# Reordering the q products of a single-head attention, with its statistics and quarter sums moved between engines

## Chip, cores and metric

The kernel runs on one core of one Trainium2 chip. The metric is the device time in microseconds (us) of one execution; the figure compared is the median of several runs. Everything is in float32.

## What is computed

The input is 8 samples of 512 channels by 1024 positions. Layer 0 is a group norm, an attention of 8 heads and an output projection, added to its input. Layer 1 takes that sum x, normalizes it over the whole sample, and does an attention with one head of 512 channels, again added to its input. The part of layer 1 that matters here is

```python
m, v = mean and variance of x over channels and positions
h = (x - m) / sqrt(v + eps) * gamma + beta
q = wq @ h + bq ;  k = wk @ h + bk ;  s = q.T @ k
```

The kernel does not form k: it multiplies x by one matrix made once from wq and wk (`wqk1`, with gamma on its rows and columns), and the product is what the code calls q. The mean and deviation of the sample enter afterwards, so the products of x can start before the statistics of x are known. The values are treated likewise with a product of wo and wv (`wvo1`).

## The kernel before

All samples go through the same stages one after the other. The program is written out by hand for three engines: TensorE (the matmuls), ScalarE and VectorE take their instructions in the order in which the code issues them (`manual_schedule`). Stages are generators that yield once for each product, and `at_steps(generator, hooks)` calls further work at numbered steps of it; a hook's instructions are thus put into each engine's order behind those of its step. GpSimd's and the sync engine's (SP's) instructions are placed by the framework's scheduler.

**Products by sevens.** A product of matrices split 2x2 is done with seven half-size products instead of eight (Strassen's way). The left factor gives A11, A12, A22 and the sums S1 to S4, the right one B11, B21, B22 and T1 to T4. `finish` (L195) and `Combined.make` (L436, 128x1024 subtractions on VectorE, 1.22 us each) make the S and T of weights and of x. Some of the half-size products are split by sevens again, into quarter products; their sums are made by `sums_a` (L513) for weights and by `quarters_in_steps` and `quarters_b` (L530, L536) for x and its T: per block one subtraction of 128x512 and two of 128x256.

**The projection of layer 0** (`project`, from L1257) computes four chunks of 128 channels by two halves of the positions, in ten steps; two chains, c = 0 and 1, alternate. Its half-size products are the matmuls `ps_p` at L679; a product of one chain is four rows of 128x512 in the profile. ScalarE copies a product to SBUF (`u_p`, L461), VectorE adds the next one to it (L1284) and adds the result with the bias to x (L1267). Behind some of these additions ScalarE passes twice over the 128x512 block of x just done for its mean and its sum of squares (`norm.moments`, L335): six of the eight blocks here, each right behind its addition in ScalarE's order, the other two in the next stage. `ready.halve("B22")` hangs on step 7 and `ready.halve("B21")` on the addition of chunk 3, half 0.

**Layer 1's q** (`make_q`, L1350 on) follows. It has six half-size products, called lines here: A11·B11, S2·T2 and S3·T3 for two column groups r = 0 and 1 (L679 `ps_l_q`, four matmuls of 128x512), and 14 quarter products (L1373, four matmuls of 128x256): seven named f for A12·B21 + S4·B22, seven named s for S1·T1 + A22·T4. A line owns one PSUM tile of two banks of pool "o" for the whole stage and uses its first bank; the quarter products take turns in two banks of pool "s". ScalarE copies (L1377) or VectorE adds (L1361) each quarter product. `take(r)` (L1394) adds the first line's bank to the f sums, `c12_of(r)` (L1398) adds the bank once S2·T2 is in it, and `final` (L1388) and one ScalarE pass (L1432) write q. The order of the products is

```
line0 A11, f0, f1, line1 A11, f2 .. f6, line0 S2, line1 S2, s0 .. s6, line0 S3, line1 S3
```

The statistics of the sample are put together meanwhile. `both_halves` (L352 to L358) is a chain of small operations on GpSimd, `mean_of_all` a tiny matmul (L307, `ps_m`) with a VectorE reduction (L309) and three GpSimd operations (L365 to L369), `deviation` another tiny matmul (`ps_v`), a VectorE operation (L374) and one on GpSimd (L375). The two tiny matmuls take a bank of their own (`room`).

**The values** (`ps_s_v`, `ps_o_v` at L937, `ps_l_v` at L694) come next, with the weights `w_wvo` and their quarter sums loaded by DMA (`WeightTwice("wvo1")`).

**The head, sample 0 only.** `wqk1` is scaled by gamma in place by eight VectorE operations (`scale_both`, L241), then gets its S sums (`finish`, L195) and its quarter sums (L513, `wqk_twice`), between the q, k and v products of layer 0. The last of these are spread over the v products by the list `over`. `waiting[0].finish` does the S sums of the first v weights, which VectorE begins once they are loaded.

Of the kernel before, what the change touches and what calls it, by code (L numbers as in the profile page):

```python
# [46 lines left out]
P = 128  # L47
# [18 lines left out]
def two_attention_blocks(  # L66
# [133 lines left out]
    class Weight:  # L200
# [34 lines left out]
                for _, a in self.moving(cc):  # L235
                    nc.scalar.activation(a, a, AF.Identity, scale=vec[:, by + cc : by + cc + 1])

        def scale_both(self, by, row):
            for cc in range(NC):
                for to, a in self.moving(cc):  # L240
                    nc.vector.scalar_tensor_tensor(  # L241
                        a, a, vec[:, by + cc : by + cc + 1], row[:, to], ALU.mult, ALU.mult
                    )

        def finish(self):
            for parts, rest in zip(self.parts, self.rest):
# [273 lines left out]
            engine.tensor_tensor(q[f"T{n}"], q[x], q[y], ALU.subtract)  # L520
        return q

    def quarters_in_steps(part, t):

        q = {f"B{n}": v for n, v in halve(part, lambda i, j: (i, j)).items()}
        t = (t if len(t.shape) == 2 else flat(t)).rearrange("p (n q) -> p n q", n=4)
        q.update({f"T{n + 1}": t[:, n, :] for n in range(4)})

        def first():
            nc.vector.tensor_tensor(  # L530
                t[:, 0:4:2, :], part[:, :, 2 * P :],
                part[:, 0, :].rearrange("p (n q) -> p n q", n=2), ALU.subtract,
            )

        def rest(n, x, y):
            nc.vector.tensor_tensor(q[n], q[x], q[y], ALU.subtract)  # L536

        return q, [first, lambda: rest("T2", "B22", "T1"), lambda: rest("T4", "B21", "T2")]

    def quarters_b(part, t):  # L540

        q, steps = quarters_in_steps(part, t)
        for step in steps:
            step()
        return q
# [5 lines left out]
    class WeightTwice:  # L551
# [3 lines left out]
        def __init__(self, name, make=None, later=None):  # L555
            tiles = [flat(tile2(f"{name}_twice_{n}")) for n in range(2)]
            key, self.tiles = f"{name}_twice", tiles
            if make is None:

                nc.scalar.dma_start(tiles[0], stored[key][:, : 8 * P])  # L560
                nc.scalar.dma_start(tiles[1], stored[key][:, 8 * P :])
                return
            stored[key] = dram.tile([P, 16 * P], FP, tag=key, name=f"stored_{key}")

            def step(n, i, a):
                sums_a(self.quarters(a, make), tiles[n][:, i * 4 * P : (i + 1) * 4 * P])
# [387 lines left out]
    def layer0(bs, qs, ks, b, norm_next):  # L954
# [302 lines left out]
        bias = made["bias0"]  # L1257

        later, ready = [], Ready(xs, b)

        def project(w, c):
            def done(i, half, bank, u):
                chunk = c + 2 * i
                x = piece(xs, chunk, half)

                def add():
                    nc.vector.scalar_tensor_tensor(  # L1267
                        x, bank if u is None else u, bias[:, chunk : chunk + 1], x, ALU.add, ALU.add
                    )
                    if i == half or i == 1:  # L1270
                        norm.moments(chunk, half, i == half)
                    if (i, half, c) == (1, 0, 1):
                        ready.halve("B21")


                first = last and i == half == 0
                if first and c == 0:
                    ps_sum = spares[0]
                    add_keys(end, [1], ps_sum)
                    combine1()  # L1280
                    combine2(2, 0)
                    combine2(3, 0)
                if u is not None:
                    nc.vector.tensor_tensor(u, bank, u, ALU.add)  # L1284
                if not first:
                    add()
                    return
                later.append(add)
                if c == 0:
                    invs[end] = one_over(ps_sum, f"0_{b}_{end}_1")  # L1290
                    divide(end, 1, invs[end])
                else:

                    held(flat(accs[end, 1]), f"acc_0_{b}_{end}", flat(accs[end, 1]))
                    for n, k in [(2, 1), (3, 1), (4, 0), (4, 1)]:
                        combine2(n, k)
                    for more in later:
                        more()

            return strassen(by_channels(w, c, comb), done, f"p_0_{b}_{c}")  # L1300

        w = next_weight().parts[0]
        hooks = {} if last else {2 * n - 3: [lambda n=n: combine2(n, 1)] for n in range(2, 5)}
        hooks[0] = [ready.load]
        hooks[7] = [lambda: ready.halve("B22")]
        at_steps(together(project(w, 0), project(w, 1)), hooks)
        if last:
            held(invs.pop(end), f"inv_0_{b}_{end}_1")
# [2 lines left out]
    class Ready:  # L1311


        def __init__(self, xs, b):
            self.combine, self.quarters, self.b = Combined(f"1_{b}"), {}, b
            self.combine.take(xs)

        def load(self):
            self.weights = WeightTwice("wqk1")

        def halve(self, name):
            self.quarters[name] = quarters_b(
                self.combine.parts[name], tile2(f"{name}_twice_{self.b}")
            )

    def attention1(xs, norm, ready, b, at_values):
# [23 lines left out]
        def make_q(w):  # L1350
# [4 lines left out]
            lines = [banks("o", f"ps_l{r}_q_1_{b}")[:, 0, :] for r in range(2)]  # L1355

            def pair(products, to, name):
                line, single = (banks("s", f"ps_{name}{n}_q_1_{b}")[:, 0, :] for n in range(2))
# [22 lines left out]
                    yield  # L1381

            def multiply(r, a, v, fresh):
                by_channels(w.parts[0], r, bs)(lines[r], a, v, fresh)

            def final(r, i, half, x, y):
                n = r + 2 * i
# [3 lines left out]

            def take(r):
                c11 = first[r][:, 0, :]
                nc.vector.tensor_tensor(c11, lines[r], c11, ALU.add)  # L1394

            def c12_of(r):
                c12 = first[r][:, 1, :]
                nc.vector.tensor_tensor(c12, lines[r], c12, ALU.add)  # L1398

            quarters = pair(PAIRS_Q[0], first, "f")  # L1400

# [21 lines left out]
            quarters = pair(PAIRS_Q[1], second, "s")  # L1423
            for n in range(7):
                next(quarters)
                if n == 2:
                    c12_of(0)
                if n == 4:
                    c12_of(1)
                yield  # L1430
            for r in range(2):
                nc.scalar.activation(  # L1432
                    piece(qs, r, 0), first[r][:, 0, :], AF.Identity, bias=norm.c[:, r : r + 1]
                )
                final(r, 0, 1, second[r][:, 0, :], first[r][:, 1, :])
            for r in range(2):
                multiply(r, "S3", "T3", False)
                for n, half in enumerate([1, 0]):
                    final(r, 1, half, lines[r], second[r][:, n, :])
                yield  # L1440
# [12 lines left out]
        bias = norm.bias()  # L1453

# [392 lines left out]
    made, throughs, over = {}, [], []  # L1847


    with tc.manual_schedule(engines={PE, ACT, DVE}):  # L1850
# [13 lines left out]
        gamma_row = tile2("gamma_row")[:, 0, :]  # L1864
        nc.sync.dma_start(gamma_row, gamma1.to_broadcast([P, C]))

        class Through(Rows):

# [15 lines left out]
                        nc.vector.tensor_tensor(t, t, vec[:, V_NW1 : V_NW1 + NC], ALU.mult)  # L1884

        def through_v():
            throughs.append(Through(wvo1, bias_v, wo1, "v", room("rows_v", 0)))
            wvo1.scale_rows(V_NW1, range(1))

        def through_q():  # L1890
            throughs.append(Through(wqk1, bias_q, nk1, "q", room("rows_q", 0)))
            wqk1.scale_both(V_NW1, gamma_row)

        def channels_of(half, ccs):
            for cc in ccs:
# [464 lines left out]
```

## Time and profile before

Times before are the median of 3 runs, from 2837.11 to 2839.54.

| | |
|---|---|
| median time | 2837.94 us |
| the profiled execution's own time | 2840.35 us |
| its span in the profile | 2838.6 us |
| granted TensorE clock, mean | 0.999 |
| VectorE busy | 2136.5 us, 75% |
| ScalarE busy | 1166.5 us, 41% |
| GpSimd busy | 299.3 us, 11% |
| projection of the second sample | 594.2 to 619.6 us |
| its q | 619.6 to 644.0 us |
| its values' weight products | 644.0 to 667 us |

The windows in the last three rows were read off the timeline. In them the engines were busy as follows (us):

| | length | TensorE | VectorE | ScalarE | GpSimd |
|---|---|---|---|---|---|
| projection | 25.4 | 24.45 | 14.67 | 10.06 | 0.00 |
| q | 24.4 | 24.35 | 21.94 | 11.31 | 4.75 |
| values | 23.0 | 23.00 | 16.96 | 4.68 | 0.00 |

How to read it: PE is TensorE, PEld its weight loads, DVE is VectorE, ACT ScalarE, POOL GpSimd. A line of the timeline has the start, the duration, the engine, the line of the kernel and the operation with output and inputs; "x4" joins four instructions, and the bracket says how long the engine had been idle and what released it. Matmuls overlap one another and their ends are modelled, so a group's duration runs over the start of the next one.

### The profile page before, as it was taken

The numbers are of one execution on the slowest core, as the hardware profiler recorded it, in microseconds if no ns is written. First come the engines' busy times: TensorE is split into PE (matmuls) and PEld (weight loads), VectorE is DVE, ScalarE is ACT, GpSimd is POOL, SyncE is SP. The second block draws the span as 40 slices with busy tenths as digits, with TensorE's granted clock in tenths as the row PEclk, the third lists the DMA queues.
The fourth block names the chain that finished last, engine by engine and source line by source line (L and its number), as shares of the span: only waits on it lengthen the run. The fifth ranks groups of instructions, "written<-read, shape, count | busy, mean of one in ns | idle before, by whom it ended". The sixth has DMA issues, their size and how long they took to land.

```text
span 2838.6 us, 39373 instructions
## 1 busy us (share of the span) xinstructions
PE 2817.4 (99%) x15688; PEld 1582.2 (56%) x15688; DVE 2136.5 (75%) x2963; ACT 1166.5 (41%) x1752; POOL 299.3 (11%) x316
## 2 busy tenths in 40 slices
PE   9999999999999999999999999999999999999999
PEld 5435765357643576445773466734667346673375
DVE  6776796767867778776777777777777777867777
ACT  2464224633256332553325533264332643326522
POOL 0000220003100040000400004000040000400021
PEclk9999999999999999999999999999999999999999
DMA  8523131331323313133131231313212142121001
GB/s 287 184 75 104 49 128 64 87 104 53 112 68 90 100 69 106 53 91 123 56 108 49 83 123 56 108 49 101 105 64 100 50 124 82 64 105 38 23 16 39
DMA packets 83864, 247.50 MB, mean 87 GB/s; under 512 B 21816, under 2 KB 22616, under 8 KB 77272
## 3 DMA queue, kind: packets, MB, share of 16 engines
q1 hardware_dynamic: 73768, 209.75, 22.5%
q10 hardware_dynamic: 9904, 35.16, 3.8%
q8 instruction: 125, 2.05, 0.3%
q14 instruction: 67, 0.55, 0.1%
HBM read 188.02 MB, written 33.03 MB: 78 GB/s over the span
## 4 chain that ended last, share of the span: by engine, by line
PE 85%; DVE 9%; DMA 3%; ACT 1%; issue 1%; SPq 0%; ACTq 0%; DVEq 0%
PE s L991 15%; PE ps_o L1010 15%; PE ps_o L1674 7%; PE ps_v L694 7%; PE ps_l_qk L916 4%; PE ps_l L1510 4%; PE ps_s L1493 4%; PE ps_s_qk L909 3%; PE ps_l_q L679 3%; PE ps_l_v L694 3%; PE ps_s L1510 3%; PE ps_o_qk L909 3%; PE ps_s_v L937 2%; PE ps_s_q L1373 2%; PE ps_p L679 2%; PE ps_s_two L1804 2%
## 5 line engine op out<-in xcount | busy, mean ns | idle before, releaser
L845 ACT ACTIVATE p<-s 128x1024 f32<-128x1024 f32 x512 | 523.3, 1024 | 329.6 <-PE s L991 322.7
L847 DVE TENSOR_TENSOR acc<-acc,p 128x1024 f32<-128x1024 f32 x384 | 469.8, 1223 | 99.7 <-ACT p L845 91.3
L1010 PE MATMUL ps_o<-p,v 64*64 64x512 f32 x4096 | 529.0, 589 | 0.0
L991 PE MATMUL s<-c_q,c_k 64*64 64x512 f32 x3584 | 465.3, 591 | 0.0
L1010 PEld LDWEIGHTS ps_o<-p,v 64*64 64x64 f32 x4096 | 156.7, 133 | 282.8 <-issue 278.0
L991 PEld LDWEIGHTS s<-c_q,c_k 64*64 64x64 f32 x3584 | 134.7, 133 | 253.2 <-issue 236.1
L1674 PE MATMUL ps_o<-t_p,s_v 128*128 128x512 f32 x384 | 168.2, 595 | 0.0
L352 POOL TENSOR_TENSOR part<-part,stat 128x4 f32<-128x4 f32 x8 | 3.6, 454 | 1443.6 <-ACT mean L335 1443.6
L847 DVE TENSOR_TENSOR acc<-p,p 128x1024 f32<-128x1024 f32 x64 | 78.3, 1224 | 79.2 <-ACT p L845 79.2
L1484 ACT ACTIVATE p<-p,factor 128x512 f32<-128x512 f32 (+1 forms) x112 | 85.3, 780 | 115.9 <-DVE p L1520 91.4
L1498 ACT COPY p<-ps_s 128x512 f32<-128x512 f32 x96 | 53.1, 588 | 178.3 <-PE ps_s L1493 178.3
L1674 PEld LDWEIGHTS ps_o<-t_p,s_v 128*128 128x128 f32 x384 | 72.4, 190 | 91.2 <-issue 89.1
L679 PE MATMUL ps_p<-t_p,w_p 128*128 128x512 f32 x256 | 114.7, 596 | 8.3 <-DVE u_p L1284 6.7
L1520 DVE TENSOR_TENSOR p<-ps_l,p 128x512 f32<-128x512 f32 x136 | 89.9, 683 | 39.9 <-PE ps_l L1510 39.6
L461 ACT COPY u_v<-ps_v 128x512 f32<-128x512 f32 x48 | 28.1, 585 | 205.4 <-PE ps_v L694 173.3
L1520 DVE TENSOR_TENSOR p<-ps_s,p 128x512 f32<-128x512 f32 x112 | 74.8, 685 | 37.7 <-PE ps_s L1510 37.7
L694 PE MATMUL ps_v<-w_v,t_again 128*128 128x256 f32 x448 | 99.0, 379 | 0.0
L694 PEld LDWEIGHTS ps_v<-w_v,t_again 128*128 128x128 f32 x448 | 85.2, 190 | 11.5
L1284 DVE TENSOR_TENSOR u_p<-ps_p,u_p 128x512 f32<-128x512 f32 x48 | 33.0, 687 | 76.5 <-ACT u_p L461 76.5
L679 PEld LDWEIGHTS ps_p<-t_p,w_p 128*128 128x128 f32 x256 | 48.0, 190 | 72.7 <-issue 54.2
L694 PE MATMUL ps_v<-w_v,x 128*128 128x256 f32 x384 | 86.8, 379 | 0.0
L679 PE MATMUL ps_p<-o,w_p 128*128 128x512 f32 x192 | 86.7, 594 | 0.0
(501 smaller groups left out, 5087.3 us busy)
## 6 DMA issues: line engine op xcount, KB each, us to landing
x<-in_x SPq DMA_DIRECT2D x92, 512.0 KB, 6.5
w_qk<-stored_qk SPq DMA_DIRECT2D x14, 1792.0 KB, 7.1
w_wqk<-stored_wqk SPq DMA_DIRECT2D x8, 1792.0 KB, 7.2
fold<-acc SPq DMA_DIRECT2D x56, 256.0 KB, 3.1
qk_twice<-stored_qk_twice ACTq DMA_DIRECT2D x28, 512.0 KB, 6.0
w_wvo<-stored_wvo SPq DMA_DIRECT2D x8, 1792.0 KB, 8.9
out<-x SPq DMA_DIRECT2D x28, 512.0 KB, 4.8
w_v<-stored_v SPq DMA_DIRECT2D x7, 1792.0 KB, 7.1
```

What stands on the lines that cost most here:

```text
L679: nc.tensor.matmul(bank, w[a][:, k, c * P : (c + 1) * P], bs[b][:, k, :], start=fresh and k == 0, stop=k == 1, skip_group_check=True,)
L694: nc.tensor.matmul(bank[:, u * 2 * P : (u + 1) * 2 * P], bs[b][:, k, n * P : (n + 1) * P], w[a][:, k, :], start=fresh and u == k == 0, sto ...
L845: nc.scalar.activation(p, s, AF.Exp, scale=factor)
L847: nc.vector.tensor_tensor(acc, first, p, ALU.add)
L909: nc.tensor.matmul(bank[:, i * 2 * P : (i + 1) * 2 * P], parts[a][x], twice_b[v][y], start=start and i == 0, stop=True, skip_group_check=True,
L916: nc.tensor.matmul(bank, of(i, a)[:, k, :], bs[v][:, k, :], start=start and k == 0, stop=k == 1, skip_group_check=True,)
L991: nc.tensor.matmul(s[cols, j, :], ks[pair][k0 // HALF][rows, k0 % HALF : k0 % HALF + HD], qs[pair][g][rows, :], start=True, stop=True,)
L1010: nc.tensor.matmul(o[cols, half, :], vs[kt][rows, c0 : c0 + HD], p[rows, j, :], start=kt == 0, stop=kt == NT - 1,)
L1493: nc.tensor.matmul(bank, bs[v][:, k, t * P : (t + 1) * P], q_parts[a][:, k, :], start=a == "A11" and k == 0, stop=k == 1, skip_group_check ...
L1510: nc.tensor.matmul(bank[:, u * 2 * P : (u + 1) * 2 * P], v[y][:, u * P : (u + 1) * P], a[x], start=start and u == 0, stop=True, skip_group ...
L1520: nc.vector.tensor_tensor(at(r, t), bank, at(r, t), ALU.add)
L1674: nc.tensor.matmul(bank, v_parts[kt // 2][a][:, kt % 2, c * P : (c + 1) * P], p_parts[kt // 2][b][:, kt % 2, cols], start=fresh and kt == ...
```

## The change

- Statistics: `done` no longer passes over x behind each addition. The pass is put on a list (`due`), and `ready.measure(n)` takes n from it at the projection's steps 1, 2, 7, 8 (two), 9 (two) and q's step 1.
- Quarter sums: those of B22, B21 and T1 are done by GpSimd; T1's at q's step 2 (was 9). T4's stay on VectorE, at step 8 (was 10).
- The T blocks of x: T1 and T2 at q's step 1 (were 2 and 3), T3 at 3 (was 12).
- q's order: the lines stand between the quarter products,

```
line0 A11, f0, f1, line1 A11, f2, f3, f4, line0 S2, f5, f6, line0 S3, s0, s1, s2, line1 S2, s3 .. s6, line1 S3
```

- The tiny matmuls of mean and deviation use the second bank of the lines' tiles. The mean is taken at step 8 (was 9), the deviation at 11 (was 10), the weights of the values' quarter sums are loaded at step 10 (was 8), `both_halves` moves from 3 to 2.
- Head: `wqk1` is scaled by ScalarE (rows) and GpSimd (columns), its quarter sums that were put off go to GpSimd, the load of the gamma row is issued at another place, and the S sums of the first v weights come ahead of those of `wqk1`.

```diff
-        def scale_both(self, by, row):
+        def scale_columns(self, row):
             for cc in range(NC):
                 for to, a in self.moving(cc):
-                    nc.vector.scalar_tensor_tensor(
-                        a, a, vec[:, by + cc : by + cc + 1], row[:, to], ALU.mult, ALU.mult
-                    )
+                    nc.gpsimd.tensor_tensor(a, a, row[:, to], ALU.mult)
...
-                sums_a(self.quarters(a, make), tiles[n][:, i * 4 * P : (i + 1) * 4 * P])
+                sums_a(
+                    self.quarters(a, make), tiles[n][:, i * 4 * P : (i + 1) * 4 * P],
+                    nc.vector if later is None else nc.gpsimd,
+                )
...
-                    if i == half or i == 1:
-                        norm.moments(chunk, half, i == half)
+                    due.append(lambda: norm.moments(chunk, half, i == half))
...
-        hooks[0] = [ready.load]
-        hooks[7] = [lambda: ready.halve("B22")]
+        for n, counts in [(1, 1), (2, 1), (7, 1), (8, 2), (9, 2)]:
+            hooks.setdefault(n, []).append(lambda n=counts: ready.measure(n))
+        hooks[2].append(ready.load)
+        hooks[7].append(lambda: ready.halve("B22"))
...
+        def measure(self, n):
+            for _ in range(n):
+                self.due.pop(0)()
...
-        def halve(self, name):
+        def halve(self, name, engine=nc.gpsimd):
             self.quarters[name] = quarters_b(
-                self.combine.parts[name], tile2(f"{name}_twice_{self.b}")
+                self.combine.parts[name], tile2(f"{name}_twice_{self.b}"), engine
             )
...
             yield from line(1, "A11", "B11", True)
-            for n in range(5):
-                next(quarters)
-                if n == 0:
-                    take(0)
-                if n == 4:
-                    take(1)
-                yield
+            yield from some(quarters, 2)
+            take(0)
+            yield from some(quarters, 1)
             yield from line(0, "S2", "T2", False)
+            c12_of(0)
+            yield from some(quarters, 2)
+            yield from line(0, "S3", "T3", False)
+            take(1)
+            quarters = pair(PAIRS_Q[1], second, "s")
+            yield from some(quarters, 3)
             yield from line(1, "S2", "T2", False)
...
+            yield from some(quarters, 1)
+            c12_of(1)
+            yield from some(quarters, 2)
...
+            finals(0)
+            yield from some(quarters, 1)
+            multiply(1, "S3", "T3", False)
+            finals(1)
+            yield
...
-            1: [lambda: norm.moments(0, 1, False)],
-            2: [lambda: combine.make(1), lambda: norm.moments(1, 1, False)],
-            3: [lambda: combine.make(2), norm.both_halves],
+            1: [lambda: ready.measure(1), lambda: combine.make(1), lambda: combine.make(2)],
+            2: [lambda: ready.halve("T1"), norm.both_halves],
+            3: [lambda: combine.make(3)],
             6: [lambda: combine.make(4)],
-            8: [lambda: twice_w.append(WeightTwice("wvo1"))],
-            9: [norm.mean_of_all, lambda: ready.halve("T1")],
-            10: [norm.deviation, lambda: ready.halve("T4")],
-            12: [lambda: combine.make(3)],
-            14: [norm.untaken],
+            8: [lambda: spare(1), norm.mean_of_all, lambda: ready.halve("T4", nc.vector)],
+            10: [lambda: twice_w.append(WeightTwice("wvo1"))],
+            11: [lambda: spare(0), norm.deviation],
+            15: [norm.untaken],
...
-            7: [wqk1.finish], 8: [waiting[0].finish], 9: [
+            7: [waiting[0].finish], 8: [wqk1.finish], 9: [
```

More of the change, by code (lines that the diff above doesn't have):

```diff
@@ L521, in sums_b, with quarters_in_steps @@
         return q
-    def quarters_in_steps(part, t):
+    def quarters_in_steps(part, t, engine=nc.vector):
         q = {f"B{n}": v for n, v in halve(part, lambda i, j: (i, j)).items()}
@@ L529, in first @@
         def first():
-            nc.vector.tensor_tensor(
+            engine.tensor_tensor(
                 t[:, 0:4:2, :], part[:, :, 2 * P :],
@@ L535, in rest, with quarters_b @@
         def rest(n, x, y):
-            nc.vector.tensor_tensor(q[n], q[x], q[y], ALU.subtract)
+            engine.tensor_tensor(q[n], q[x], q[y], ALU.subtract)
         return q, [first, lambda: rest("T2", "B22", "T1"), lambda: rest("T4", "B21", "T2")]
-    def quarters_b(part, t):
-        q, steps = quarters_in_steps(part, t)
+    def quarters_b(part, t, engine=nc.vector):
+        q, steps = quarters_in_steps(part, t, engine)
         for step in steps:
@@ L1259, in layer0 @@
         later, ready = [], Ready(xs, b)
+        due = ready.due
         def project(w, c):
@@ L1316, in __init__ @@
             self.combine.take(xs)
+            self.due = []
+        def measure(self, n):
+            for _ in range(n):
+                self.due.pop(0)()
         def load(self):
             self.weights = WeightTwice("wqk1")
-        def halve(self, name):
+        def halve(self, name, engine=nc.gpsimd):
             self.quarters[name] = quarters_b(
-                self.combine.parts[name], tile2(f"{name}_twice_{self.b}")
+                self.combine.parts[name], tile2(f"{name}_twice_{self.b}"), engine
             )
@@ L1354, in make_q @@
             first, second = ([tile2(f"{n}_q_1_{b}_{r}") for r in range(2)] for n in ["c11", "c22"])
-            lines = [banks("o", f"ps_l{r}_q_1_{b}")[:, 0, :] for r in range(2)]
             def pair(products, to, name):
@@ L1383, in multiply @@
             def multiply(r, a, v, fresh):
-                by_channels(w.parts[0], r, bs)(lines[r], a, v, fresh)
+                by_channels(w.parts[0], r, bs)(lines[r][:, 0, :], a, v, fresh)
             def final(r, i, half, x, y):
@@ L1393, in take, with finals @@
                 c11 = first[r][:, 0, :]
-                nc.vector.tensor_tensor(c11, lines[r], c11, ALU.add)
+                nc.vector.tensor_tensor(c11, lines[r][:, 0, :], c11, ALU.add)
             def c12_of(r):
                 c12 = first[r][:, 1, :]
-                nc.vector.tensor_tensor(c12, lines[r], c12, ALU.add)
+                nc.vector.tensor_tensor(c12, lines[r][:, 0, :], c12, ALU.add)
+            def finals(r):
+                final(r, 0, 1, second[r][:, 0, :], first[r][:, 1, :])
+                for n, half in enumerate([1, 0]):
+                    final(r, 1, half, lines[r][:, 0, :], second[r][:, n, :])
             quarters = pair(PAIRS_Q[0], first, "f")
@@ L1413, in make_q @@
             yield from line(1, "A11", "B11", True)
-            for n in range(5):
-                next(quarters)
-                if n == 0:
-                    take(0)
-                if n == 4:
-                    take(1)
-                yield
-            yield from line(0, "S2", "T2", False)
-            yield from line(1, "S2", "T2", False)
[L1423 to L1430, printed above, removed]
+            yield from some(quarters, 2)
+            take(0)
+            yield from some(quarters, 1)
+            yield from line(0, "S2", "T2", False)
+            c12_of(0)
[4 more added lines that the diff above has]
+            yield from some(quarters, 3)
+            yield from line(1, "S2", "T2", False)
+            yield from some(quarters, 1)
+            c12_of(1)
+            yield from some(quarters, 2)
             for r in range(2):
@@ L1434, in make_q, with spare @@
                 )
[L1435 to L1440, printed above, removed]
+            finals(0)
[3 more added lines that the diff above has]
+            yield
+            spares.clear()
+        def spare(r):
+            spares[:] = [lines[r][:, 1, :]]
+        lines = [banks("o", f"ps_l{r}_q_1_{b}") for r in range(2)]
         at_steps(make_q(w), {
-            1: [lambda: norm.moments(0, 1, False)],
-            2: [lambda: combine.make(1), lambda: norm.moments(1, 1, False)],
-            3: [lambda: combine.make(2), norm.both_halves],
+            1: [lambda: ready.measure(1), lambda: combine.make(1), lambda: combine.make(2)],
+            2: [lambda: ready.halve("T1"), norm.both_halves],
+            3: [lambda: combine.make(3)],
             6: [lambda: combine.make(4)],
-            8: [lambda: twice_w.append(WeightTwice("wvo1"))],
-            9: [norm.mean_of_all, lambda: ready.halve("T1")],
-            10: [norm.deviation, lambda: ready.halve("T4")],
-            12: [lambda: combine.make(3)],
-            14: [norm.untaken],
+            8: [lambda: spare(1), norm.mean_of_all, lambda: ready.halve("T4", nc.vector)],
+            10: [lambda: twice_w.append(WeightTwice("wvo1"))],
+            11: [lambda: spare(0), norm.deviation],
+            15: [norm.untaken],
         })
@@ L1845, in all_good @@
         nc.vector.tensor_copy(flag, ps[0:1, 0:1])
-    made, throughs, over = {}, [], []
+    made, throughs, over, gamma_row = {}, [], [], []
     with tc.manual_schedule(engines={PE, ACT, DVE}):
@@ L1863, in two_attention_blocks @@
         norm = norm0(xs_next, 0)
-        gamma_row = tile2("gamma_row")[:, 0, :]
-        nc.sync.dma_start(gamma_row, gamma1.to_broadcast([P, C]))
         class Through(Rows):
@@ L1886, in through_v @@
         def through_v():
+            gamma_row.append(tile2("gamma_row")[:, 0, :])
+            nc.sync.dma_start(gamma_row[0], gamma1.to_broadcast([P, C]))
             throughs.append(Through(wvo1, bias_v, wo1, "v", room("rows_v", 0)))
@@ L1891, in through_q @@
             throughs.append(Through(wqk1, bias_q, nk1, "q", room("rows_q", 0)))
-            wqk1.scale_both(V_NW1, gamma_row)
+            wqk1.scale_rows(V_NW1)
+            wqk1.scale_columns(gamma_row[0])
         def channels_of(half, ccs):
```

## The prediction

> **What bounds the kernel now.** I read the page's busy shares and its chain first:
>
> ```profile
> PE 2817.4 (99%) x15688; PEld 1582.2 (56%) x15688; DVE 2136.5 (75%) x2963; ACT 1166.5 (41%) x1752; POOL 299.3 (11%) x316
> ...
> PE 85%; DVE 9%; DMA 3%; ACT 1%; issue 1%; SPq 0%; ACTq 0%; DVEq 0%
> ```
>
> TensorE is the bound and GpSimd nearly idle. The matmuls stay the same in number and shape, so only time in which TensorE stands still can be won. Second, the table of TensorE's waits (total us, times, longest):
>
> ```profile
> PE ps_p L679 <- DVE u_p L1284: 6.7, 7, 1.2
> PE ps_l_v L694 <- DVE c_v L630: 2.0, 1, 2.0
> ...
> PE ps_l_q L679 <- DVE u_p L1284: 0.9, 6, 0.2
> ```
>
> The first row is the projection, the third the seam from it to q; both are stages the change edits. Since ends of matmuls are modelled, I size stalls by the starts of PE rows instead. In an unbroken stretch four 128x512 passes take 1.715 us (614.18 to 615.89), 0.429 each; quarter passes (128x256) come to 0.216. The second sample's projection is 56 passes, 24.04 us dense, but lasts 594.18 to 619.64, 25.46. Its q is 24 x 0.429 + 56 x 0.216 = 22.39 dense, but lasts 24.38. So 1.42 and 1.99 us are lost per sample. Third, the timeline of the larger hole:
>
> ```profile
> 601.05 1.88 PE L679 MATMUL ps_p<-t_p,w_p 128*128 128x512 f32 x4
> ...
> 601.50 0.72 ACT L335 ACTIVATE square<-x,stat 128x512 f32<-128x512 f32 x1
> ...
> 602.41 0.58 ACT L461 COPY u_p<-ps_p 128x512 f32<-128x512 f32 x1
> 603.03 0.69 DVE L1284 TENSOR_TENSOR u_p<-ps_p,u_p 128x512 f32<-128x512 f32 x1 [2.38 <-ACT u_p L461]
> ...
> 603.77 1.55 PE L679 MATMUL ps_p<-t_p,w_p 128*128 128x512 f32 x3 [0.84 <-DVE u_p L1284]
> ```
>
> The copy that frees the bank sits behind mean and square of x (600.75 to 602.32), its add behind it, TensorE behind the add. The next product should start 1.715 us after 601.05 (602.77, less a late step of the modelled start); start by start I find 1.11 us lost here. Fourth, VectorE at the end of the projection:
>
> ```profile
> 616.72 0.69 DVE L530 TENSOR_TENSOR B_twice<-x 128x512 f32<-128x512 f32 x1
> 617.44 0.89 DVE L536 TENSOR_TENSOR B_twice<-x,B_twice 128x256 f32<-128x256 f32 x2
> 618.24 0.75 DVE L1267 SCALAR_TENSOR_TENSOR x<-ps_p,bias,x 128x512 f32<-128x512 f32 x1
> 618.90 0.68 DVE L1284 TENSOR_TENSOR u_p<-ps_p,u_p 128x512 f32<-128x512 f32 x1
> ```
>
> B22's quarter sums hold back the add for which q's first product waits. Fifth, TensorE in q:
>
> ```profile
> 619.64 1.98 PE L679 MATMUL ps_l_q<-x,w_wqk 128*128 128x512 f32 x4 [0.15 <-DVE u_p L1284]
> ...
> 623.34 1.98 PE L679 MATMUL ps_l_q<-x,w_wqk 128*128 128x512 f32 x4
> ...
> 628.84 1.13 PE L1373 MATMUL ps_f_q<-B_twice,w_wqk 128*128 128x256 f32 x4
> ...
> 633.64 0.39 PE L307 MATMUL ps_v<-spread,in_sample 128*128 128x4 f32 x2
> ```
>
> A group that comes late shows some 0.1 us of extra duration. The holes before these groups: 0.32 (plus 0.10 in the first pass), 0.25, 0.26, 0.50; smaller ones of 0.08 to 0.24 make the rest of the 1.99.
>
> **The statistics on ScalarE.** Removed from ahead of the copies: a pair of passes, 1.57 us (600.75 to 602.32). With the new order ScalarE's copy can start right after the product, 5.35 us into the projection, and its add ends at about 7.75, while TensorE needs it at 8.58: the hole goes. Over samples 0 to 6 it is 1.24, 1.11, 1.12, 0.96, 1.45, 1.30, 1.36, sum 8.5. In the last sample ScalarE's order still has two pairs ahead of the copy, so its 1.26 us hole stays, as do 0.95 us behind the reciprocal. The passes themselves cost nothing where they go: ScalarE is busy 10.1 of 25.4 us in this stage. But what is queued behind them is q's copies at steps 8, 9 and 1; at 0.58 us each they come every 0.86 us or slower, so I take zero. If that cover is gone, a product that reuses the bank waits up to 1.57 once per sample.
>
> **Quarter sums to GpSimd.** B22, B21 and T1 leave VectorE: 0.69 + 0.89, some 1.5 us each. B22's removal takes the 0.32 us at the seam: 8 x 0.32 = 2.5. Together with B21's it also takes q's first 0.10 and the 0.25 before the second half-size product, whose add is then ready about 0.95 us into q, against 3.44. On GpSimd one set is 1.27 (128x512, its row by shape) + 2 x 0.73 = 2.73 us. B21's are then ready 1.3 to 2.7 us into q, and needed at 5.16. T1's come behind B21's, and ahead of both_halves on GpSimd's queue: the means are there at 8.2 to 8.7, needed by the mean's matmul at 10.3. Margin 1.6 at worst, cost zero; that matmul is in TensorE's queue, so a miss stops everything behind it.
>
> **The new order of q.** VectorE, from q's start: the last four adds of the projection (about 0.68 each when queued), T1 and T2 (1.16 each), an add (0.6), T3 (1.16), then the take (0.7): 7.5 us. The half-size S2 product waits for that take and is due at 1.715 x 2 + 0.863 x 5 = 7.75. So 0.2 us of slack, no more. What remains in q if this holds: two tiny matmuls at 0.22 (the 0.50 at the deviation falls to that, as its GpSimd input now has longer), and 0.1, 0.08, 0.1 at reused banks, 0.73 together. The moved DMA of wvo1 (two steps later) is used after q, over 8 us later than either place, against a 6.0 us row for the like load: nothing. After q, the v stage needs the bank of VectorE's last final at 5.34 us after the last quarter product, and gets it at 5.0 to 5.2: nothing.
>
> **What GpSimd beside VectorE costs.** The trace of before has the pair only in the last sample's v stage, where GpSimd's sums of S and A lie beside VectorE's:
>
> ```profile
> 2727.85 0.94 DVE L513 TENSOR_TENSOR S_twice<-s_q 128x256 f32<-128x256 f32 x1
> ...
> 2729.59 1.20 DVE L635 TENSOR_TENSOR c_v<-c_v,c_v 128x512 f32<-128x512 f32 x1
> ...
> 2731.45 4.57 PEld L694 LDWEIGHTS ps_l_v<-w_wvo,t 128*128 128x128 f32 x14 [2.35 <-DVE c_v L630]
> ```
>
> Alone these take 0.42 and 0.69; beside GpSimd each is about 0.5 longer, and TensorE waited 2 us. The Trainium skill, SBUF — State Buffer, section "SBUF: two separate sides", speaks against the change: VectorE with two SBUF inputs and GpSimd share a port pair as an exclusive lock, the loser blocked for the other's whole instruction. By the rule the two sets inside q (5.46 us), less 1.2 beside sums read from PSUM (L1520's 0.68 is not longer near GpSimd), block VectorE for 4.3 us. By the row it is 0.5 us for each VectorE sum that overlaps. Exposed at the take are T2 and T3: by the row 0 to 1.0, less the 0.2 of slack, 0.8 at the S2 product; by the rule 4.1. I side with the row, since it is the same pair of operations, and take its middle, 0.4, with 0.05 for the quarter product before it. A gain is excluded. So q loses 0.73 + 0.45 = 1.18 per sample, 9.6 over eight (rounded up), from 7 x 1.99 + 2.65 = 16.6 before. Gain 7.0; 10.7 with no contention.
>
> **The head, once.** Scaling wqk1 leaves VectorE (8 x 0.40 = 3.2 us) and the wqk_twice sums too (16 x 0.27 = 4.3), but the latter stood behind the v add (67.30) for which TensorE waited 0.5 us. Now w_v's finish (2.5 us) stands ahead of wqk1's in VectorE's queue and waits for the load that before was issued at 54.8 and landed at 60.4; it is issued somewhat earlier, so I estimate 57.3 to 59.9. From landing, two finishes, the adds and the qk sums end 10.9 later with the v add: 68.2 to 70.8, where it ended at 67.98. Six c_q issues now pass ahead on SP (about 1.1 us each there), inside that estimate. Bounds -0.6 and +7 (3.8 of it blocking by GpSimd's wqk sums); I take +2.
>
> **Sum.** -8.5 - 2.5 - 7.0 + 2 = -16. The profiled execution took 2840.35 (span 2838.6), the median run 2837.94. 2840.35 - 16 = 2824; in terms of the median 2822.
>
> **The rivals.** No contention: GpSimd's sums fall beside adds from PSUM. -8.5 - 2.5 - 10.7 + 0 = -21.7, 2816. For it: most of VectorE's work there reads PSUM. Against: three 1024-wide combines lie exactly under T1's sums.
>
> Half given back: VectorE's chain slips 1.2 us per sample, q gains nothing, the head loses 3: -8, 2830. For it: 0.2 us of slack at the take.
>
> Slower, one mechanism: the lock in full. T1's GpSimd sums block T2 or T3, the take comes 4.3 us late, and TensorE stands 4.1 before the S2 product in each sample. q then loses 8 x (0.73 + 4.1) = 38.6, 22 more than before: -11 + 22 + 2 = +13, 2851. It decides from a stall of about 2.5 us per sample there (q then eats the 11 - 2 won elsewhere). Against: the rows show 0.5 a sum, not whole instructions.
>
> Or the change doesn't do what it says: each hole reopens behind the next wait on the same bank, 2837. Against: the walk leaves 0.8 us at the large hole.
>
> **Chances.** Likeliest case 0.60 (2816 to 2828), no contention 0.14, half given back 0.15, hole reopens 0.06, slower 0.05. A measurement can tell about 0.2%, 5.7 us, from no change: faster is below 2832.3. Half given back lies mostly below it, and the reopened holes within: faster 0.87, same 0.08, slower 0.05. Range 2811 to 2831: the likeliest, most of no contention and about half of half given back, 0.8.
>
> **What would show it.** Right: the row of ps_p behind u_p shrinks to about one wait (the last sample's), projection lengths near 24.1 us, q near 23.5, VectorE's combines in q at 1.2 to 1.7. Wrong: a new row of ps_l_q waiting for DVE c_q, or ps_l_q behind POOL stat; combines above 2; ps_v waiting over 2 us at 68 to 71.

## The result, and the profile after

The changed kernel takes 2828.71 us (median of 8 runs, 2827.51 to 2830.19); in the same series the kernel before takes 2838.61 (8 runs, 2836.96 to 2841.15). The ratio is 0.9965, with a 95% interval of 0.9954 to 0.9976: 9.9 us faster, clear of no change, and inside the forecast range. The forecast was 16 us. The profiled executions took 2840.35 before and 2828.29 after (spans 2838.6 and 2825.7), so what follows explains 12.9 us of span.

The table of TensorE's waits, after (total us, times, longest), is the first view to set beside the one of before:

```profile
PE ps_v L695 <- DVE v L729: 4.3, 1, 4.3
PE ps_l_v L695 <- DVE c_v L631: 1.9, 1, 1.9
PE ps_q L680 <- DVE q L712: 1.8, 1, 1.8
...
PE ps_p L680 <- ACT u_p L459: 1.2, 1, 1.2
...
PE ps_v L695 <- DVE q L712: 0.9, 1, 0.9
```

The rows of the projection and of q behind VectorE are gone; the last sample's wait for ScalarE's copy stays. But three rows, each occurring once, are new or grown (`ps_v` behind `v` was 0.2 us before): they belong to the head of sample 0, and together are 7.0 us. (Lines moved by the change: L680 here is L679 before, L1285 is L1284, L1380 is L1373.)

The sum by stages, each measured from the first matmul of one to the first of the next (us, all samples; dense length as in the prediction):

| stage | idle or slow before | after | difference |
|---|---|---|---|
| projections, 8 | 12.8 | 2.4 | -10.5 |
| q, 8 | 16.6 | 7.6 | -9.0 |
| values of the last sample | 3.7 | 2.0 | -1.7 |
| head, to the first projection (start at 246.36, then 255.02) | | | +8.7 |
| sum | | | -12.5 |

That leaves 0.4 us elsewhere. The row of the values is a difference of the granted clock between two executions, and no gain of the change (shown further down); without it the stages give -10.8, against the medians' -9.9. Each projection of samples 0 to 6 now lasts 24.03 us (one, the third, 24.51), each q 23.33 (the last 23.38). The timeline of ScalarE in the second sample's projection shows why:

```profile
605.57 0.58 ACT L459 COPY u_p<-ps_p 128x512 f32<-128x512 f32 x1 [2.85 <-PE ps_p L680]
606.95 0.63 ACT L333 ACTIVATE mean<-x 128x512 f32<-128x512 f32 x1 [0.79 <-DVE x L1269]
```

The copy starts as soon as TensorE has released the bank, and mean and square come behind it. TensorE in the same window, as two rows without a bracket, did not stop:

```profile
603.65 3.60 PE L680 MATMUL ps_p<-o,w_p 128*128 128x512 f32 x8
607.09 4.45 PE L680 MATMUL ps_p<-t_p,w_p 128*128 128x512 f32 x10
```

The busy time of the engines over q of that sample, after (columns: length, then TensorE, weight loads, VectorE, ScalarE, GpSimd with their counts, granted clock, DMA share and GB/s):

```profile
624.25:647.58 23.33, 23.33 (x86) 15.32 (x85) 18.37 (x29) 9.18 (x20) 10.73 (x17) 1.00 0.35 124
```

In q VectorE fell from 21.94 to 18.37 and GpSimd rose from 4.75 to 10.73. VectorE's and GpSimd's rows at the start of that q show what the two do to each other:

```profile
626.22 1.63 DVE L434 TENSOR_TENSOR t<-x,x 128x1024 f32<-128x1024 f32 x1
627.89 1.23 DVE L434 TENSOR_TENSOR t<-x,t 128x1024 f32<-128x1024 f32 x1
629.03 0.68 DVE L1368 TENSOR_TENSOR c_q<-ps_f_q,c_q 128x512 f32<-128x512 f32 x1
629.64 1.84 DVE L434 TENSOR_TENSOR t<-x,x 128x1024 f32<-128x1024 f32 x1
631.40 0.68 DVE L1401 TENSOR_TENSOR c_q<-ps_l_q,c_q 128x512 f32<-128x512 f32 x1
```

```profile
624.92 1.86 POOL L534 TENSOR_TENSOR B_twice<-x,B_twice 128x256 f32<-128x256 f32 x2
628.32 0.86 POOL L350 TENSOR_TENSOR part<-part,stat 128x4 f32<-128x4 f32 x1 [1.54 <-ACT mean L333]
629.13 1.27 POOL L528 TENSOR_TENSOR T_twice<-t 128x512 f32<-128x512 f32 x1
630.36 1.21 POOL L352 TENSOR_SCALAR part<-part 128x4 f32<-128x4 f32 x1
```

T1 (626.22) runs beside the end of B21's sums and takes 1.63 instead of 1.22; T3 (629.64) beside T1's sum takes 1.84. T2 takes 1.23: beside it GpSimd has only a small 128x4 operation that starts later (628.32). That operation pays instead: it takes 0.86 us, the one at 630.36 takes 1.21, where others of this size take 0.20, and each ends within 0.1 us of the VectorE sum beside it (which end at 629.12 and 631.48). The adds that read PSUM stay at 0.68. The take ends at 632.08, and the S2 product, due at 632.0, starts at 632.13, about 0.1 us late.

The head is the other side. VectorE before, two of its rows:

```profile
50.94 0.28 DVE L513 TENSOR_TENSOR wvo_twice<-w_wvo 128x128 f32<-128x128 f32 x1
...
60.37 0.69 DVE L195 TENSOR_TENSOR w_v<-rest_v,w_v 128x512 f32<-128x512 f32 x1 [1.10 <-DMA w_v<-in_s_v]
```

and after the change, four rows:

```profile
51.46 0.81 DVE L511 TENSOR_TENSOR wvo_twice<-w_wvo 128x128 f32<-128x128 f32 x1
...
56.37 0.74 DVE L712 SCALAR_TENSOR_TENSOR q<-ps_q,vec,u_q 128x512 f32<-128x512 f32 x1
...
61.84 0.69 DVE L195 TENSOR_TENSOR w_v<-rest_v,w_v 128x512 f32<-128x512 f32 x1 [4.06 <-DMA w_v<-in_s_v]
...
71.74 0.54 DVE L511 TENSOR_TENSOR qk_twice<-w_qk,qk_twice 128x128 f32<-128x128 f32 x1
```

and GpSimd beside them:

```profile
50.62 2.97 POOL L241 TENSOR_TENSOR w_wqk<-w_wqk,gamma_row 128x256 f32<-128x256 f32 x4
...
71.63 0.50 POOL L511 TENSOR_TENSOR wqk_twice<-wqk_twice,w_wqk 128x128 f32<-128x128 f32 x1
```

The 16 wvo_twice sums, 3.8 us in all before (50.94 to 54.75), take 7.9 (48.53 to 56.45) next to GpSimd's scaling and first sums of wqk1. The last of them also releases the load of w_v (issued 54.78 before, 56.48 after), so its S sums start at 61.84 and not at 60.37. wqk1's S sums, which before filled most of the time until that load landed, now come behind it, and the 16 qk_twice sums, 3.7 us before, take 5.7. Then the granted clock (columns as above):

```profile
75.18:77.00 1.82, 1.82 (x4) 1.52 (x5) 1.82 (x4) 0.00 (x0) 0.00 (x0) 0.50 0.67 132
77.00:79.00 2.00, 2.00 (x8) 1.62 (x7) 1.10 (x2) 0.00 (x0) 0.00 (x0) 0.68 0.87 286
```

After its 4.3 us of waiting TensorE ran 1.8 us at 0.50 and 2.0 us at 0.68 of its clock. That is 1.82 x 0.50 + 2.00 x 0.32 = 1.6 us more, which no row of waits shows; in the next 2 us the clock is back at 1.00.

### The profile page after: what moved, and what is told of

The parts are those of the page before. It is cut to its first block, busy times and chain, and to the rows that moved or that the text cites. A ratio compares the mean times of both kernels' runs of the same rounds, so it can differ in the third digit from the quotient of the medians.

```text
span 2825.7 us, 39407 instructions
## 1 busy us (share of the span) xinstructions
PE 2806.3 (99%) x15688; PEld 1585.4 (56%) x15688; DVE 2114.7 (75%) x2867; ACT 1171.2 (41%) x1760; POOL 394.3 (14%) x412
## 4 chain that ended last, share of the span: by engine, by line
PE 92%; DVE 6%; issue 1%; DMA 0%; ACT 0%; ACTq 0%; POOL 0%; DVEq 0%; POOLq 0%
PE s L992 16%; PE ps_o L1011 16%; PE ps_o L1686 7%; PE ps_v L695 7%; PE ps_p L680 6%; PE ps_l_qk L917 5%; PE ps_l L1522 4%; PE ps_s L1505 4%; PE ps_s_qk L910 4%; PE ps_l_q L680 3%; PE ps_l_v L695 3%; PE ps_s L1522 3%; PE ps_o_qk L910 3%; PE ps_s_v L938 2%; PE ps_s_q L1380 2%; PE ps_s_two L1816 2%
## 5 line engine op out<-in xcount | busy, mean ns | idle before, releaser
L528 POOL TENSOR_TENSOR B_twice<-x 128x512 f32<-128x512 f32 x16 | 20.4, 1274 | 1353.8 <-DVE x L1269 1353.3
L680 PE MATMUL ps_p<-t_p,w_p 128*128 128x512 f32 x256 | 112.8, 593 | 1.8 <-ACT u_p L459 1.2
L373 POOL TENSOR_TENSOR rstd<-rstd,minus_half 128x4 f32<-128x4 f32 (+1 forms) x16 | 12.8, 798 | 567.3 <-DVE rstd L372 567.3
L680 PE MATMUL ps_p<-o,w_p 128*128 128x512 f32 x192 | 86.9, 594 | 0.2 <-DVE o L1031 0.2
L680 PEld LDWEIGHTS ps_p<-t_p,w_p 128*128 128x128 f32 x256 | 48.5, 190 | 63.7 <-issue 59.1
```

Source lines behind the costliest of these rows:

```text
L680: nc.tensor.matmul(bank, w[a][:, k, c * P : (c + 1) * P], bs[b][:, k, :], start=fresh and k == 0, stop=k == 1, skip_group_check=True,)
```

## The experiments

My theory at this point: the two stages won what was to be won there, and the head, edited in passing, took 8.7 us of it back. The rival: the head's delay is only a shift that comes back later, or the stages are not what won. The first four runs undo the head's edits, all or one at a time; the next six take the three parts of the stage change (statistics, GpSimd's sums, q's order) in every other combination; the last two go on from what was learnt. Every ratio is to the kernel before, run beside it.

**All head edits taken back.** `scale_both`, the wqk_twice sums and the order of the S sums as before, and the load of the gamma row back in its old place (not in this cut):

```diff
-            wqk1.scale_rows(V_NW1)
-            wqk1.scale_columns(gamma_row[0])
+            wqk1.scale_both(V_NW1, gamma_row[0])
...
-                    nc.vector if later is None else nc.gpsimd,
+                    nc.vector,
...
-            7: [waiting[0].finish], 8: [wqk1.finish], 9: [
+            7: [wqk1.finish], 8: [waiting[0].finish], 9: [
```

> The changed kernel with all edits to the head taken back: wqk1 scaled by VectorE, its put-off quarter sums on VectorE, its S sums ahead of those of the first v weights, the gamma row loaded where it was. Theory (the head eats 8.7 us of what the two stages win: the first projection starts at 255.0 us after the change, 246.4 before): that start goes back to 246.4, projection and q stay as changed (24.0 and 23.3 us), time 2820, ratio 0.9935. Rival (the 8.7 is the changed scheduling of loads and comes back elsewhere, or the last sample's stages give up their gain): 2825 or more.

Measured: 2820.34, ratio 0.9932 (0.9919 to 0.9946). The first projection starts at 246.53; projections and q are as in the changed kernel. The theory holds: nothing of the 8.7 comes back later.

**One head edit at a time.** Three runs, each with one of the three edits in the cut above:

> The changed kernel with only the scaling of wqk1 back on VectorE (8 operations of 0.40 us). Theory (GpSimd's column scaling stretches the wvo_twice sums beside it from 0.20 to about 0.7 us a piece, and the add that TensorE waits for stands behind them): wvo_twice sums at 0.20 to 0.28, the 1.8 us wait of ps_q gone, the w_v load issued at 54.8 instead of 56.5; the later waits for v stay about as long. 2 us faster than the changed kernel, 2827. Rival (no port conflict, the sums were late for another reason): VectorE has 3.2 us more to do ahead of that add and the wait grows, 2830 or more.

> The changed kernel with only the put-off quarter sums of wqk1 back on VectorE, where they stand behind the v adds. Theory of port conflict: the 16 qk_twice sums ahead of the v add fall from up to 0.54 us each to 0.20 to 0.29, the v wait from 4.3 to about 2 us, and with less idle time TensorE may keep its clock (0.50 for about 2 us after the wait now, some 1.6 us lost): 2.4 to 4 us faster than the changed kernel, 2825 to 2826. Rival (the wait is only a matter of the order of the two finishes): no change, 2828.7, or slower by the VectorE time added.

> The changed kernel with only the two S-sum steps in their old order, wqk1 first. Theory (VectorE idles 4.06 us waiting for the load of w_v at 57.8 to 61.8, and wqk1's 2.9 us, which would fit in there, come behind it): the 0.9 us wait of ps_v for q goes, the v wait falls from 4.3 to about 1, the clock stays at 1.00: 6 us faster than the changed kernel, 2823. Rival (all of it is port conflict): v wait stays above 3 us, gain under 1 us.

| | time | ratio (interval) | q and k of the head | v of the head |
|---|---|---|---|---|
| before | 2838.6 to 2839.1 | 1 | 26.69 | 24.68 |
| changed | 2828.71 | 0.9965 (0.9954, 0.9976) | 28.18 | 31.64 |
| scaling on VectorE | 2827.53 | 0.9959 (0.9945, 0.9972) | 27.35 | 31.78 |
| wqk_twice on VectorE | 2823.32 | 0.9943 (0.9930, 0.9957) | 27.53 | 29.36 |
| wqk1's S sums first | 2821.84 | 0.9938 (0.9925, 0.9952) | 28.18 | 25.76 |
| all three, and the gamma row | 2820.34 | 0.9932 (0.9919, 0.9946) | 26.70 | 24.65 |

The last two columns are us from first matmul to first matmul in the profile. The order of the two S-sum steps accounts for 5.9 of the 7.0 us in the v stage: in that run wqk1's sums end at 61.1, ahead of the load, and TensorE waits 1.3 for v instead of 4.3, with its clock at 1.00. GpSimd's sums account for 2.3 there; the two overlap and don't add up. With these sums back on VectorE the wait for v fell to 2.1 us, as expected, but the clock fell all the same (0.62 and 0.53 from 72 to 76). The q and k part is contention of both GpSimd edits with VectorE (the "port conflict" of the expectations): scaling alone saves 0.83, the sums alone 0.65, together 1.48, which leaves nothing for the gamma row. The scaling run missed its 2 us: with the scaling back, wvo_twice was still slowed for three sums by GpSimd's first wqk1 sums (0.54 at 51.2), and 0.7 of the 1.8 us wait remained.

**The parts of the stage change.** The old head throughout. S is the statistics put off, G the quarter sums of B22, B21 and T1 on GpSimd, O q's new order with its hooks. S also moves a weight load, `ready.load`, two steps later; the run without S keeps it there, and the hole is back, so the load is not what closes it. The edits that take a part out or leave it alone:

```diff
-        def halve(self, name, engine=nc.gpsimd):
+        def halve(self, name, engine=nc.vector):
...
                     due.append(lambda: norm.moments(chunk, half, i == half))
+                    if i == half or i == 1:
+                        due.pop()()
```

The first takes out G, the second S (with the `measure` hooks of the projection gone and two passes at q's step 1), both together leave O alone; S alone, G alone and S with G are the kernel before plus these hunks the other way round.

> The changed kernel with the old head and the quarter sums of B22, B21 and T1 back on VectorE, at the places that the change gave them. Theory (the new order of q works only because VectorE is freed: the take comes with almost no slack): VectorE's chain to the take grows by B21's and T1's 1.5 us each, TensorE waits 2.5 to 4 us at the first S2 product of every sample, and the seam's 0.3 us comes back: 20 to 35 us slower than with GpSimd, 2842 to 2855. Rival (the port conflict costs about what the move saves): within 5 us of 2820.

> The changed kernel with the old head and the statistics of six blocks again right behind their adds (the other two in q, now together). Theory: the hole behind the copy returns in samples 0 to 6 at 1.0 to 1.5 us, 8.5 together: projection 25.1 to 25.5 long, 2828 to 2829. Rival (the hole came from VectorE's load, which GpSimd now carries): no hole, 2820.

> The kernel before with nothing but the statistics put off (due list, the same steps). Theory: the 1.0 to 1.5 us holes of samples 0 to 6 go, 8.5 us; the seam's 0.3 and q's 2.0 stay: 2830. Rival (the new place of the passes delays q's copies or the means): under 5 us gained, with new waits of ps_f_q or ps_m.

> The kernel before with nothing but the quarter sums of B22, B21 and T1 moved to GpSimd, at their old places, q in its old order. Theory: the seam's 0.32 + 0.10 and the 0.25 before the second half-size product go, 5.4 us in eight samples, the 1.1 us hole of the projection stays; at T1's old place the GpSimd sums come beside the spread operations, so the wait for the deviation may grow by up to 1 us a sample: 2833, bounds 2831 to 2841. Rival (port conflict takes it back): 2838 or more, with q longer than 24.4.

> The kernel before with q's new order alone: statistics behind their adds (the two left for q together at its second step), all quarter sums on VectorE, old head. Theory: each part needs the others. The projection keeps its 25.3 to 25.8 us, and in q the take is late by the 1.3 us that it was late with the sums on VectorE, plus what the holes of the projection push on: q 25 to 25.6 us against 24.38, 5 to 10 us slower than before, 2844 to 2849. Rival (the order by itself is a gain): q under 24.38, 2835 or less.

> The kernel before with the statistics put off and the quarter sums of B22, B21 and T1 on GpSimd, but q in its old order. Theory: the projection is dense (24.03) as with the statistics alone, and the wait for GpSimd's spread of 1.1 us a sample stays, because T1's sums still stand between the mean and the spread on GpSimd: q 24.9 to 25.3, 2831 to 2835. Rival (that wait came only from the late projection): q 24.0, 2825 or less.

| parts | time | ratio (interval) | projection 2 | q 2 |
|---|---|---|---|---|
| none (before) | 2839.1 to 2839.4 | 1 | 25.46 | 24.38 |
| S | 2824.58 | 0.9946 (0.9929, 0.9963) | 24.03 | 24.02 |
| G | 2844.86 | 1.0019 (1.0012, 1.0026) | 25.52 | 25.29 |
| O | 2852.59 | 1.0047 (1.0032, 1.0062) | 25.71 | 26.33 |
| S, G | 2835.54 | 0.9987 (0.9981, 0.9994) | 24.03 | 25.20 |
| S, O | 2831.24 | 0.9970 (0.9958, 0.9983) | 24.03 | 24.69 |
| G, O | 2833.57 | 0.9982 (0.9975, 0.9989) | 25.27 | 24.23 |
| S, G, O | 2820.34 | 0.9932 (0.9919, 0.9946) | 24.03 | 23.32 |

"Projection 2" and "q 2" are lengths in the second sample; the q of the other samples but the last differ from it by 0.02 or less. Single projections scatter more: the sixth is 1.4 to 1.6 us longer than the second in G and in S with G, for a cause left open.

Most of the gain is S: alone it wins 14.9 of the 18.8 us of all three. On top of S, G alone and O alone each lose, and only together do they bring 4 us more.

Five of the six times missed their forecast, and S with G lies 0.5 above its own. *S alone* won about 14.9 us, not 8.5: with the hole gone, the seam's 0.32 went too, and 0.36 of q, although B22's sums were still on VectorE. But *G alone* closes the seam too, with the hole still there (1.4 us): q's first product starts without a wait in all eight samples of either run. The first row is S alone, the second G alone:

```profile
616.67 1.88 PE L679 MATMUL ps_l_q<-x,w_wqk 128*128 128x512 f32 x4
...
619.53 1.88 PE L679 MATMUL ps_l_q<-x,w_wqk 128*128 128x512 f32 x4
```

In *O alone*, which has neither, the seam is 0.32 as before. *G alone* made the kernel slower, above all for one wait, found in TensorE's table and in GpSimd's rows of that run:

```profile
PE ps_v L307 <- POOL spread L369: 8.4, 8, 1.1
```

```profile
631.81 0.30 POOL L365 TENSOR_SCALAR spread<-stat,mean_m 128x4 f32<-128x4 f32 x1 [4.15 <-DVE mean_m L309]
632.08 1.26 POOL L530 TENSOR_TENSOR T_twice<-t 128x512 f32<-128x512 f32 x1
633.30 0.20 POOL L368 TENSOR_TENSOR spread<-spread 128x4 f32<-128x4 f32 x1
633.45 0.72 POOL L536 TENSOR_TENSOR T_twice<-t,T_twice 128x256 f32<-128x256 f32 x1
634.13 0.20 POOL L369 TENSOR_TENSOR spread<-spread,stat 128x4 f32<-128x4 f32 x1
```

The scheduler laid T1's sums between the spread operations, each of them 0.2 to 0.3 us, and the deviation's matmul waits 1.05 us. S with G has the same wait at the same place, so it does not come from the late projection. *S with O* lost 10.9 us to S, G, O, less than the 20 to 35 expected: TensorE waits for the take 1.3 us a sample, not 2.5 to 4.

```profile
PE ps_l_q L682 <- DVE c_q L1403: 10.1, 8, 1.3
```

VectorE had idled 0.68, 0.24 and 0.96 us at the end of the changed kernel's projection, and B21's sums fill that gap; only T1's 1.5 us hit the take. *G with O* came out 13.2 us slower than all three, not 8.5: besides the hole, q is 0.9 longer, as TensorE waits for VectorE twice in each (0.4 and 0.2 us). That VectorE enters q late behind the hole is the likely reason, not shown by itself. *O alone* is worst, 13.4 us slower than before and beyond the 5 to 10 expected: both the take (1.3) and an earlier quarter product (1.1) wait in each sample.

**Going on.** Both runs have S, G and O and the old head. In the first, the last sample's two early pairs of statistics come at step 5; the second also has the last sample's quarter sums of q (S4, A22) on VectorE:

```diff
-        for n, counts in [(1, 1), (2, 1), (7, 1), (8, 2), (9, 2)]:
+        for n, counts in [(5, 2) if last else (1, 1), (2, 0 if last else 1), (7, 1), (8, 2), (9, 2)]:
...
-        halve_a("S4", None, nc.gpsimd)
-        halve_a("A22", None, nc.gpsimd)
+        halve_a("S4", None, nc.vector if last else nc.gpsimd)
+        halve_a("A22", None, nc.vector if last else nc.gpsimd)
```

> The changed kernel with the old head, and in the last sample the first two statistics pairs three steps later, behind ScalarE's copies. Theory: the 1.2 us that TensorE waits for ScalarE's copy in the last projection goes: 2819, 1.2 faster than with the old head alone. Rival: the means come too late in the last q and TensorE waits there instead, 2820 or more.

> As the run before, and in the last sample GpSimd's quarter sums of S4 and A22 of q on VectorE, behind its other work there. Theory (beside them VectorE's sums take 0.8 to 1.5 us where they take 0.42 alone, and TensorE waits 2.0 us for c_v, after which the clock may fall to 0.5): that wait goes, 2 to 3.6 us more, 2816 to 2817. Rival (VectorE is as late with 3.3 us more to do): a wait for these sums in the last scores, no gain.

The first measured 2819.72, ratio 0.9932 (0.9918 to 0.9946): not told apart from the old head alone. In its profile the wait for ScalarE's copy fell from 1.2 to 0.8 us only, since the two pairs (2660.06 to 2663.14) then stand ahead of the next pair of copies; step 5 is still too early. The second measured 2817.69, ratio 0.9924 (0.9910 to 0.9938): 2.0 lower in median than the run beside it, with overlapping intervals. Its profile is clear: without GpSimd beside them VectorE's sums are back at 0.42, TensorE's wait for c_v is gone, and the values of the last sample last 23.09 us instead of 26.77 (2.0 of the wait, 1.7 of the clock behind it).

```profile
2707.18 0.42 DVE L513 TENSOR_TENSOR S_twice<-s_q 128x256 f32<-128x256 f32 x1
```

This is the fastest version found, 21 us ahead of the kernel before.

## Why the prediction was right, and where it was off

The direction, the likeliest mechanism and the range held: the change is faster because the waits in projection and q go. The size did not: 9.9 us instead of 16. The measured 2828.71 lies just above the band of the likeliest case (2816 to 2828) and nearer to the rival "half given back" (2830) than to 2822. That rival's mechanism, no gain in q, did not occur; q gained 9.0. So the range held by its width as much as by the sum. By stages, the holes and the seam came within 0.5 us of their 11.0, q gave 2.0 more than forecast, and the head cost 6.7 more: one mis-sized term.

- **"The head, once."** Taken at +2, with bounds of -0.6 and +7; it measured +8.7, above its bound. This is the term that failed. Three things in it: the w_v load was put earlier ("issued somewhat earlier"), while it waits for the last wvo_twice sum and was issued 1.7 later, so that w_v's sums start at 61.84, where the landing was put at 57.3 to 59.9; the scaling on GpSimd was counted as relief for VectorE (3.2 us) and not as contention for the 16 sums beside it (7.9 us for 3.8); and a loss of clock after a long wait was not counted at all (1.6). Of the head's edits, taken back one by one, the order of the two S-sum steps weighs most: wqk1's 2.9 us no longer fill the wait for the load.
- **"The statistics on ScalarE."** Right, by its own sum: 8.5 predicted, and the holes of samples 0 to 6 are gone; the last sample's wait for ScalarE's copy stayed, as said (1.2).
- **"Quarter sums to GpSimd", the seam.** The 2.5 us came, but the reason given is half of it. G alone closes the seam, as predicted; S alone closes it too, with B22's sums still on VectorE. The add was late only when both came together, VectorE held up by the hole and then given B22's sums, so the 2.5 us belong to neither edit alone. The same holds for q's first 0.10 and 0.25. What GpSimd's sums are worth is seen only under the new order: 10.9 us of take waits.
- **"The new order of q."** Predicted 7.0, measured 9.0: what is left is 0.94 a sample, not 1.18. The clean part was put at 0.73, which leaves 0.2 for contention and not 0.45. That the take came out 0.1 late, near the forecast, is luck, as two errors cancel. Of the four adds counted ahead of it, two were done before q began, so its slack, counted the same way, was about 1.2 us and not 0.2. And VectorE lost 1.3 us on the way: 0.41 and 0.62 in T1 and T3, and 0.26 in the add at 625.18.
- **"What GpSimd beside VectorE costs."** T1, T3 and T4 lost 0.41, 0.62 and 0.16 us, 1.2 a sample and not 4.3. The lock that the prediction quotes was misapplied, not refuted. At their start 0.56, 0.76 and 0.30 us of a GpSimd sum were still to run, and each lost that rest less 0.14. The changed kernel's trace has 55 VectorE sums of two SBUF operands that start at least 0.2 us before a GpSimd instruction ends; all 55 lost the rest of it less 0.13 to 0.15. So a sum waits for the one instruction under way, as under that lock, and not for all of GpSimd's sums, as the 4.3 and the slower rival assumed. In the head, where VectorE's sums alone come every 0.2 to 0.3 us, each came only every 0.6 to 0.8 beside the scaling: there contention decided.
- **The margin of the mean.** No time was lost in the new order, but the margin of 1.6 us was used up: in all eight samples GpSimd's last operation of the means ends within 0.1 us of the mean's matmul (634.87 and 634.82 in the second). T1's sums and the waits beside T2, T3 and T4 had delayed the chain. G alone shows what a miss costs, there for the deviation: with T1's sums at their old place TensorE waits 1.05 us a sample.
- **Not predicted: -1.7 in the last sample's values.** That is clock and no gain of the change. Before, after the wait for c_v, the profile grants 0.61, 0.50, 0.50 and 0.69 in four successive windows of 1 us (2732 to 2736); after, 1.00 throughout behind the same wait.

## What to carry to other kernels

A stall can need two causes, and then removing either ends it: before crediting an edit with a stall, ask whether its engine was late already, and try the parts in combination, since here they gain 14.9, lose 5.4 and lose 13.4 us alone (each against its own runs of before) and gain 18.8 together. Work for an idle engine is free only if nothing short and urgent stands beside it or behind it in that engine's queue. An edit that runs once can cost as much as one that runs eight times saves, so walk it as carefully, above all what each load waits for and what fills the time until it lands.

## What the runs showed of the hardware

A VectorE sum of two SBUF operands that meets a GpSimd instruction lost the rest of that instruction less about 0.14 us, whatever its own length, so short sums lost most in proportion. A 128x128 one came every 0.20 to 0.32 us alone and every 0.62 to 0.84 beside GpSimd's scaling (0.77 us each); a 128x1024 one went from 1.22 to 1.85 at worst; sums that read PSUM stayed at 0.68. In the trace of before 21 of 29 such meetings follow the rule; in the other eight VectorE, already ahead, lost nothing beside a 128x1 operation.

The clock fell after shorter waits than I had expected. The wait of about 2.0 us for c_v in the last sample occurs in 13 of the 14 profiles. In 6 of them the stage then lasted 26.77 us, with a granted clock of 0.50 for about 3.4 us; in 7 of them it lasted 25.08 to 25.09, with a clock of 1.00 throughout. In the head it fell after waits of 4.3 us (the changed kernel) and 2.1 (wqk_twice on VectorE), and not after one of 1.3 (wqk1's S sums first). The Trainium skill, "TensorE: Matmul & The Clock Gate", Part 1, tells of an activity window of 3.4 us that runs freely. Where the wait falls in such a window could decide, but no run here shows it; they show that 2.0 us is sometimes enough.
